# Two QKV groups of the second head pair, issued behind the first two blocks of head 0

## The chip, the cores and the metric

The kernel runs on one core of one Trainium2 chip. The metric is the device time of one execution in microseconds (us); several executions are made, and the median counts. One further execution is recorded by the hardware profiler; its trace gives every instruction of every engine with start and duration, from the first instruction of the program to the last (the span).

The core has five engines that work beside each other, each through its own queue in order: TensorE (PE; its weight loads are listed apart as PEld), VectorE (DVE), ScalarE (ACT), GpSimd (POOL) and SyncE (SP), which here only issues transfers. Matrix products land in PSUM, eight banks of 128 x 512 float32; everything else lies in SBUF.

## The reference

A transformer block on 2048 rows of 1024 features: 16 attention heads of 64 features with rotary positions and a causal mask, then a feed-forward part whose weights come as 4-bit codes with scales.

```
x = L0_attn_hidden_states                       # 1 x 2048 x 1024
x = x + layernorm(attn(layernorm(x), Wq, Wk, Wv, Wo))
x = x + layernorm(ffn(layernorm(x), gate, up, down))

attn(h):  q, k, v = h @ Wq, h @ Wk, h @ Wv      # 16 heads x 64
          q, k = rotary(q), rotary(k)
          p = softmax(causal(q @ k.T) / 8)
          return concat(p @ v) @ Wo
ffn(h):   W = NF4[codes] * scales               # 2752 x 1024, blocks of 64
          return (silu(h @ Wg.T) * (h @ Wu.T)) @ Wd.T
```

## The kernel before

**Precision.** Large products are made of float32 values split into a high part and the rest. `split` writes the high part on ACT (line 120) and the rest on DVE (line 121); `mm3` (lines 112 to 114) issues three matmuls for one product, high x high, high x rest and rest x high. A weight tile is prepared in the same manner by `prep_w`: one transfer into an "f4" buffer (line 179), a scaled cast on ACT (line 186), the rest on DVE (line 190) or POOL.

**Stages.** The 2048 rows are four column blocks c of 512. `make_x` loads, normalizes and transposes one block into four tiles `xs[c]`, and stores them to `xd` for later. A *group* (m, c) is one call of `qkv`: query, key and value (n = 0, 1, 2) of head pair m (heads 2m and 2m + 1) for block c. Each n takes 24 matmuls per 512 columns, three for each of eight row tiles, 72 for the group. The result is copied out of its bank by ACT (line 251, or 241 for the value). Queries and keys are rotated with a table `tab` on DVE and POOL (lines 253 to 256), split into `hl` and stored to `qs` or `ks`; values are transposed on PE (line 244), split into `vo` and stored to `vs`. All stores are issued by SP.

With `ramp=True` a group takes PSUM banks of kind "S" for n = 0 and 2 and "F" for n = 1, and the transfer of `tab` is issued by ACT. Without it all three take the one "F" bank, and SP issues the table. Values are always transposed in "F".

Attention goes head by head. `attend(h, J, ...)` handles 512 queries: `scores` makes J + 1 blocks of 512 keys for each of four tiles of 128 queries (two matmuls each, lines 278 and 280, in a bank of kind "S"), takes the maximum on DVE (284 or 286), the exponential on ACT (288), and scales on POOL (310); `weighted` transposes the probabilities on PE (320), splits them into `pw` and multiplies by v (324, 325). Head 0 loads its k, v and q by parts and goes through J = 0, 1, 2, 3.

**What sets the order.** The order of the instructions on each engine is fixed when the program is built. A planner works with estimated times: of the instructions that are ready, it takes the one that stands first in the program; `early` moves a helper ahead by 1000 places. So a later line of the program runs first only where an earlier one still lacks data, a buffer or a bank. Groups of pairs 2 to 7 fill PE beside attention; during pair 0, heads 0 and 1, these are (2, 0) to (2, 3). They are traced behind both heads, and `pace` ties each product to a score matmul, which it must not precede.

**Buffers.** Each kind has a fixed number: "hd" 7, "w" 3, "xc" 4, "pa" 6, "pb" 2, "f4" 4, "pw" 3, "t2" 3. Blocks 1 and 3 of x lie in "xc", block 2 in four of "hd", block 0 in four of "pa". The weights of pair 0 take the three "w", those of pair 1 two of "pa" and two of "pb". k and v of a head take one "hd" each, and q of two blocks one more. Probabilities of block J take J + 1 of "pa". `tab`, `hl`, `vo` and the raw weights `wf` take "f4"; the copies `t1` and `sh` take "t2".

**Around the change.** Lines 356 to 365 make x and the first eight groups, those of pairs 0 and 1, by `both`. Lines 398 to 401 prepare the weights of pair 2 and load x for (2, 0), ahead of the loop over J of head 0 (line 404). Line 409 takes q buffers for two blocks at a time.

Of the kernel before, what the change touches and what calls it, by code (L numbers as in the profile page):

```python
# [57 lines left out]
def block_kernel(ctx, tc, x, wq, wk, wv, wo, gu_codes, gu_scales, d_codes, d_scales, cos_sin, out):  # L58
# [15 lines left out]
    def slot(tag, shape, dtype, name):  # L74
        assert int(np.prod(shape[1:])) * 4 <= SLOTS[tag][1] * 1024, (tag, shape)
        return sb.tile(shape, dtype, tag=tag, name=name, bufs=SLOTS[tag][0])

    def bank(tag, name="bk"):
        return ps.tile([P, 512], F32, tag=tag, name=name, bufs=BANKS[tag])
# [22 lines left out]
    def f32(ap):  # L102
        return ap.bitcast(F32)

    def after(ins, other):

        dep = mybir.DependencyInfo(mybir.DependencyClass.NoSync, mybir.DependencyReason.DATA)
        tc.add_manual_dep(ins.ins, other.ins.name, dep, reason="pace")

    def mm3(o, w, xx, first, last):  # L110

        r = T.matmul(o, lhsT=w[:, 0], rhs=xx[:, 0], start=first, stop=False)  # L112
        T.matmul(o, lhsT=w[:, 0], rhs=xx[:, 1], start=False, stop=False)  # L113
        T.matmul(o, lhsT=w[:, 1], rhs=xx[:, 0], start=False, stop=last)  # L114
        return r
# [3 lines left out]
    def split(hi, lo, src):  # L119
        high[:] = [A.copy(hi, src)]  # L120
        return V.tensor_tensor(lo, src, f32(hi), ALU.subtract)  # L121
# [96 lines left out]
    def load_x(c):  # L218
        tiles = []
        for kp in range(4):  # L220
            tiles.append(slot("xc", [P, 2, 2, 512], FR, "xc"))
            load(f32(tiles[kp]), xd[c][:, kp])
        return tiles

    def prep_qkv(m, tags=("w", "w", "w")):
        behind = (None, high[-1], high[-1]) if m == 0 else (None,) * 3
        return [prep_w(w, m, sc, tag, b) for w, sc, tag, b in zip((wq, wk, wv), (0.125, 1.0, 1.0), tags, behind)]

    def qkv(m, c, ws, xs, ramp=False, pace=None):
        cs = slice(c * 512, (c + 1) * 512)  # L230
        tab = slot("f4", [P, 2, 512], F32, "tab")
        (A.dma_start if ramp else load)(tab, cos_sin[:, :, cs])
        for n, w in enumerate(ws):
            o = bank("S" if ramp and n != 1 else "F", "qkv")
            for k in range(KE):
                mm = mm3(o, w[k], xs[k // 2][:, :, k % 2, :], k == 0, k == KE - 1)
                if k == 0 and pace:
                    pace(mm, n)
            t1 = slot("t2", [P, 512], F32, "t1")
            if n == 2:  # L240
                A.copy(t1, o)
                pv = bank("F", "pv").rearrange("p (t n) -> p t n", t=4)
                for t in range(4):
                    T.transpose(pv[:, t, :], t1[:, t * P : (t + 1) * P], ident)
                vo = slot("f4", [P, 4, 2, 2, D], FR, "vo")
                src = pv.rearrange("p t (a d) -> p t a d", a=2)
                for a in range(2):
                    split(vo[:, :, a, 0, :], vo[:, :, a, 1, :], src[:, :, a, :])
                load(vs[m][cs].rearrange("(t p) a n -> p t (a n)", p=P), f32(vo.rearrange("p t a l d -> p t (a l d)")))
            else:  # L250
                A.copy(t1, o)
                sh = slot("t2", [P, 512], F32, "sh")
                V.stream_shuffle(sh, t1, [i ^ 1 for i in range(32)])
                V.tensor_tensor(t1, t1, tab[:, 0, :], ALU.mult)
                G.tensor_tensor(sh, sh, tab[:, 1, :], ALU.mult)
                G.tensor_tensor(t1, t1, sh, ALU.add)
                hl = slot("f4", [P, 2, 512], FR, "hl")
                split(hl[:, 0, :], hl[:, 1, :], t1)
                load((qs, ks)[n][m][:, :, cs], f32(hl))
# [71 lines left out]
    def load_kv(h, k, v, cs):  # L331

        m, r = h // 2, h % 2 * D
        for a in range(2):
            load(f32(k[a * D : (a + 1) * D, cs]), ks[m][r : r + D, a, cs])
        load(f32(v[:, cs.start // P : cs.stop // P]), vs[m][cs, h % 2, :].rearrange("(t p) n -> p t n", p=P))

    def load_q(h, q, J):

        m, r = h // 2, h % 2 * D  # L340
        for a in range(2):
            load(f32(q[a * D : (a + 1) * D]), qs[m][r : r + D, :, J * 512 : J * 512 + 512])

    def early(f, *args):
        tc.trace_state.cur_priority -= EARLY
        r = f(*args)
        tc.trace_state.cur_priority += EARLY
        return r

    xs = [early(make_x, 0)]  # L350
    first = [early(prep_qkv, 0), prep_qkv(1, ("pa", "pa", "pb"))]

    def new_x(c):
        xs.append(early(make_x, c))

    def both(*steps):
        for m, c in steps:
            qkv(m, c, first[m], xs[c], ramp=True)
# [3 lines left out]
    new_x(2)  # L362
    both((0, 1), (1, 1))
    new_x(3)
    both((0, 2), (0, 3), (1, 2), (1, 3))

    def new_kv():
        return slot("hd", [P, S], FR, "k"), slot("hd", [P, NT, P], FR, "v")

    def new_q():  # L370

        q = slot("hd", [P, 2, 2, 512], FR, "q")
        return [q[:, 0], q[:, 1]]

    def attend(h, J, q, k, v, anchors):
        weighted(h, J, scores(J, q, k, anchors), v)
# [7 lines left out]
    def group(m, c, xs=None, pace=None):  # L384
        if m not in ws:
            ws[m] = prep_qkv(m)
        qkv(m, c, ws[m], xs or load_x(c), pace=pace)

    for pair in range(KE - 1):
        anchors = []  # L390
        now = [later[g] for g in range(len(later)) if g * (KE - 1) // len(later) == pair]
        own = now and now[0][0] == pair
        for h in (2 * pair, 2 * pair + 1):
            k, v = new_kv()
            by_part = h == 0 or (own and h % 2 == 0)
            if not by_part:
                load_kv(h, k, v, every)
            if h % 2 == 0 and not own:
                if now[0][0] not in ws:
                    ws[now[0][0]] = prep_qkv(now[0][0])  # L400
                ready = load_x(now[0][1])
            order = FIRST if by_part else ORDER
            qj = {}
            for i, J in enumerate(order):
                if by_part:
                    if own and J == now[0][1]:
                        group(*now.pop(0))
                    load_kv(h, k, v, parts[J])
                if i % 2 == 0:
                    two = order[i : i + 2]  # L410
                    qj.update(zip(two, new_q()))
                    for jj in () if by_part else two:
                        load_q(h, qj[jj], jj)
                if by_part:
                    load_q(h, qj[J], J)
                attend(h, J, qj[J], k, v, anchors)
        for i, (m, c) in enumerate(now):

            def pace(mm, n):
                want = PACE * (3 * i + n) / (3 * len(now)) * anchors[-1][0]  # L420
                after(mm, next(a for a in anchors if a[0] >= want)[1])

            group(m, c, None if i or own else ready, pace)
# [416 lines left out]
```

## Time and profile before

| what | us |
|---|---|
| median of three executions | 3017.91 |
| the executions | 3012.16, 3017.91, 3018.10 |
| profiled execution, its own time | 3014.01 |
| its span, first to last instruction | 3012.1 |
| mean granted TensorE clock | 0.991 of full |

Costly groups, from the page (line, engine, operation, output<-inputs, shape, count | busy us, mean ns of one | idle us before them, and what ended most of it):

```profile
L288 ACT ACTIVATE prob<-s,mxs 128x512 f32<-128x512 f32 (+3 forms) x640 | 402.6, 632 | 147.8 <-DVE mxs L286 90.6
...
L320 PE MATMUL pt<-ident,prob 128*128 128x128 f32 x2176 | 345.5, 275 | 6.8 <-DVE pw L121 5.5
...
L286 DVE TENSOR_REDUCE mxs<-s 128x1 f32<-128x512 f32 x384 | 260.9, 681 | 60.0 <-PE s L280 59.1
...
L112 PE MATMUL qkv<-xc,w 128*128 128x512 f32 x576 | 231.8, 402 | 10.3 <-ACT w L186 6.3
```

The operand `qkv<-xc,w` marks the groups whose x was loaded again; the first eight groups read `xr`, the tiles as they were made. Matmuls overlap in PE's pipeline, so the mean duration of one is longer than the distance between two starts. The page divides the span into 40 slices of 75.3 us and gives for each the busy share of each engine in tenths, and the clock that TensorE was granted. The trace further answers for any stretch of time: busy time of each engine, what ended each wait, and the single instructions in order.

### The profile page before, as it was taken

To read this page: it belongs to the slowest core of one execution; us is meant where nothing else is said; L and a number is where in the kernel's file an instruction comes from. 1 tells how busy PE (TensorE), PEld (TensorE's weight loads), DVE (VectorE), ACT (ScalarE), POOL (GpSimd) and SP (SyncE) were. 2 spreads that over 40 slices of the span, in tenths; PEclk is the share of its full clock that TensorE was granted. 3 is DMA by queue.
4 is the path that set the end of the run, shared out by engine and by line. 5 is a ranking of instruction groups with operands and counts; after the bars stand their busy time and mean duration, and the time that the engine had idled before them with its cause. 6 is when DMAs were issued, how large, how long until landed. Compare 5 with 4: busy or idle time off the path is not lost.

```text
span 3012.1 us, 42532 instructions
## 1 busy us (share of the span) xinstructions
PE 2917.0 (97%) x14168; PEld 2409.7 (80%) x14168; DVE 2035.8 (68%) x4171; ACT 1698.4 (56%) x3569; POOL 953.0 (32%) x1055
## 2 busy tenths in 40 slices
PE   7989999999998999999999999999999999999998
PEld 6868888787887787777788788888888887888887
DVE  6567778886777778777665767776666677444347
ACT  4256667776666667667555655655555566333234
POOL 4344344443434343445322121222211223100034
PEclk9999999999999999999999999999999999999999
DMA  8787665757556468463456444444334444744446
GB/s 287 277 249 233 214 222 177 222 161 220 172 195 182 146 202 260 137 210 105 123 187 213 130 134 143 151 133 140 131 119 140 138 153 146 254 141 148 150 144 234
DMA packets 271740, 536.01 MB, mean 178 GB/s; under 512 B 22944, under 2 KB 113056, under 8 KB 255648
## 3 DMA queue, kind: packets, MB, share of 16 engines
q1 hardware_dynamic: 269344, 529.10, 54.6%
q10 hardware_dynamic: 2176, 4.19, 0.4%
q8 instruction: 112, 1.84, 0.3%
q14 instruction: 108, 0.88, 0.1%
HBM read 371.98 MB, written 161.22 MB: 177 GB/s over the span
## 4 chain that ended last, share of the span: by engine, by line
PE 79%; DMA 10%; DVE 4%; ACT 2%; POOL 2%; issue 1%; SPq 1%; POOLq 0%; ACTq 0%; DVEq 0%
PE bk L112 14%; PE bk L114 14%; PE bk L113 14%; PE pt L320 6%; PE qkv L112 4%; PE qkv L113 4%; PE qkv L114 4%; PE o L325 3%; PE o L324 3%; PE s L278 3%; PE s L280 3%; DMA wf<-in_wq 3%; PE pj L469 2%; PE pj L471 2%; PE pj L470 2%
## 5 line engine op out<-in xcount | busy, mean ns | idle before, releaser
L310 POOL TENSOR_SCALAR prob<-prob,rc 128x512 f32<-128x512 f32 (+3 forms) x640 | 405.4, 659 | 436.4 <-DVE rc L305 219.6
L112 PE MATMUL bk<-x,wt 128*128 128x512 f32 x1376 | 534.0, 390 | 2.7 <-ACT wt L120 1.8
L113 PE MATMUL bk<-x,wt 128*128 128x512 f32 x1376 | 535.2, 389 | 0.0
L114 PE MATMUL bk<-x,wt 128*128 128x512 f32 x1376 | 535.1, 389 | 0.0
L288 ACT ACTIVATE prob<-s,mxs 128x512 f32<-128x512 f32 (+3 forms) x640 | 402.6, 632 | 147.8 <-DVE mxs L286 90.6
L121 DVE TENSOR_TENSOR pw<-pt,pw 128x512 fp32r<-128x512 f32 (+3 forms) x640 | 378.4, 602 | 119.7 <-ACT pw L120 118.0
L534 ACT ACTIVATE ln<-cs,bias 128x512 f32<-128x512 f32 x520 | 360.0, 716 | 109.2 <-DVE m L541 25.4
L120 ACT CAST pw<-pt 128x512 fp32r<-128x512 f32 (+3 forms) x640 | 324.1, 527 | 171.6 <-PE pt L320 140.6
L320 PE MATMUL pt<-ident,prob 128*128 128x128 f32 x2176 | 345.5, 275 | 6.8 <-DVE pw L121 5.5
L320 PEld LDWEIGHTS pt<-ident,prob 128*128 128x128 f32 x2176 | 267.6, 141 | 61.7 <-issue 7.2
L112 PEld LDWEIGHTS bk<-x,wt 128*128 128x128 f32 x1376 | 258.2, 188 | 57.5 <-ACT wt L120 2.6
L286 DVE TENSOR_REDUCE mxs<-s 128x1 f32<-128x512 f32 x384 | 260.9, 681 | 60.0 <-PE s L280 59.1
L114 PEld LDWEIGHTS bk<-x,wt 128*128 128x128 f32 x1376 | 258.3, 188 | 53.8
L113 PEld LDWEIGHTS bk<-x,wt 128*128 128x128 f32 x1376 | 258.3, 188 | 53.5
L278 PE MATMUL s<-k,q 128*128 128x512 f32 (+3 forms) x640 | 265.7, 416 | 25.1 <-ACT prob L288 22.4
L325 PE MATMUL o<-pw,v 128*128 128x512 f32 (+3 forms) x640 | 247.3, 388 | 9.5 <-DVE pw L121 9.0
L324 PE MATMUL o<-pw,v 128*128 128x512 f32 (+3 forms) x640 | 244.3, 382 | 9.8 <-ACT pw L120 7.9
L112 PE MATMUL qkv<-xc,w 128*128 128x512 f32 x576 | 231.8, 402 | 10.3 <-ACT w L186 6.3
L113 PE MATMUL bk<-bt,at 128*128 128x512 f32 x616 | 239.6, 389 | 0.0
L114 PE MATMUL bk<-bt,at 128*128 128x512 f32 x616 | 238.8, 389 | 0.0
L112 PE MATMUL bk<-bt,at 128*128 128x512 f32 x616 | 238.7, 389 | 0.0
L280 PE MATMUL s<-k,q 128*128 128x512 f32 (+3 forms) x640 | 236.6, 372 | 0.0
(150 smaller groups left out, 5513.8 us busy)
## 6 DMA issues: line engine op xcount, KB each, us to landing
xc<-xd SPq DMA_DIRECT2D x96, 1024.0 KB, 9.3
q<-qs SPq DMA_DIRECT2D x128, 256.0 KB, 7.2
ast<-S SPq DMA_DIRECT2D x44, 512.0 KB, 3.9
cs<-in_gu_scales SPq DMA_DIRECT2D x172, 128.0 KB, 3.2
cs<-in_gu_codes SPq DMA_DIRECT2D x86, 256.0 KB, 3.0
A<-in SPq DMA_DIRECT2D x66, 256.0 KB, 2.0
S<-in SPq DMA_DIRECT2D x66, 256.0 KB, 3.2
ast<-A SPq DMA_DIRECT2D x33, 512.0 KB, 4.5
```

Source lines behind the costliest of these rows:

```text
L112: r = T.matmul(o, lhsT=w[:, 0], rhs=xx[:, 0], start=first, stop=False)
L113: T.matmul(o, lhsT=w[:, 0], rhs=xx[:, 1], start=False, stop=False)
L114: T.matmul(o, lhsT=w[:, 1], rhs=xx[:, 0], start=False, stop=last)
L121: return V.tensor_tensor(lo, src, f32(hi), ALU.subtract)
L278: mm = T.matmul(s, lhsT=q[:, 0, j * P : (j + 1) * P], rhs=k[:, b:e], start=True, stop=False)
L280: T.matmul(s, lhsT=q[:, 1, j * P : (j + 1) * P], rhs=k[:, b:e], start=False, stop=True)
L288: A.activation(prob[i][:, j, : e - b], s, AF.Exp, bias=mx, scale=sign, accum_out=sums[:, j % BATCH, i : i + 1])
L310: G.tensor_scalar(p, p, rc[:, jj % BATCH, i : i + 1], 0.0, ALU.mult, ALU.add)
L320: T.transpose(pt[:, j * P : (j + 1) * P], prob[kb // 4][:, j, kb % 4 * P : (kb % 4 + 1) * P], ident)
L324: T.matmul(o[:, cs], lhsT=v[:, kb, :], rhs=pw[:, 0, cs], start=kb == 0, stop=False)
L325: T.matmul(o[:, cs], lhsT=v[:, kb, :], rhs=pw[:, 1, cs], start=False, stop=kb == nk - 1)
L534: A.activation(ln, c8, AF.Prelu, bias=bias_of[ab], scale=ab[0], alpha=ab[2])
```

## The change

The groups (1, 2) and (1, 3) are taken out of the last call of `both` and called inside the loop over J of head 0, before its third block. There they are called without `ramp=True`, so that all three products take the "F" bank and SP issues the table.

```diff
@@ -362,7 +362,7 @@
     new_x(2)
     both((0, 1), (1, 1))
     new_x(3)
-    both((0, 2), (0, 3), (1, 2), (1, 3))
+    both((0, 2), (0, 3))
 
     def new_kv():
         return slot("hd", [P, S], FR, "k"), slot("hd", [P, NT, P], FR, "v")
@@ -402,6 +402,10 @@
             order = FIRST if by_part else ORDER
             qj = {}
             for i, J in enumerate(order):
+                if h == 0 and i == 2:
+
+                    for c in (2, 3):
+                        qkv(1, c, first[1], xs[c])
                 if by_part:
                     if own and J == now[0][1]:
                         group(*now.pop(0))
```

The arithmetic and the number of instructions stay as they were.

## The prediction

> **What bounds the kernel now.** I read the page first: busy time, then the forty slices.
>
> ```profile
> PE 2917.0 (97%) x14168; PEld 2409.7 (80%) x14168; DVE 2035.8 (68%) x4171; ACT 1698.4 (56%) x3569; POOL 953.0 (32%) x1055
> ...
> PE   7989999999998999999999999999999999999998
> ...
> PE 79%; DMA 10%; DVE 4%; ACT 2%; POOL 2%; issue 1%; SPq 1%; POOLq 0%; ACTq 0%; DVEq 0%
> ```
>
> TensorE is busy 97% of 3012.1 us, and 79% of the chain of waits is PE. The change removes no arithmetic, so it can only gain where PE stands still or runs at a lowered clock. After the start, the only 8 among the first twelve slices is the fourth (150.6 to 225.9 us). So next I asked for the busy time of the engines in stretches around it (columns: stretch, length, busy us and count of PE, weight loads, DVE, ACT, POOL, granted clock, DMA share, GB/s).
>
> ```profile
> 100.00:168.00 68.00, 67.57 (x316) 55.68 (x314) 25.22 (x52) 17.67 (x41) 23.77 (x16) 1.00 0.79 262
> ...
> 204.00:268.00 64.00, 63.99 (x343) 53.62 (x342) 46.54 (x109) 39.36 (x102) 29.57 (x38) 1.00 0.72 229
> ```
>
> Up to 168 us PE is full of QKV products while DVE works 25 of 68 us. From 204 us on, attention and later QKV groups fill it again. The hole lies between:
>
> ```profile
> 168.00:172.00 4.00, 1.50 (x6) 0.88 (x6) 2.55 (x9) 2.25 (x8) 0.00 (x0) 0.96 1.02 238
> 172.00:176.00 4.00, 4.00 (x11) 2.83 (x12) 1.66 (x7) 1.45 (x4) 1.99 (x4) 0.61 1.14 246
> 176.00:180.00 4.00, 4.00 (x20) 3.28 (x19) 0.00 (x0) 0.30 (x1) 0.10 (x1) 1.00 1.09 271
> 180.00:184.00 4.00, 1.68 (x11) 1.17 (x9) 2.01 (x5) 1.61 (x4) 3.04 (x2) 1.00 1.05 300
> 184.00:188.00 4.00, 3.15 (x11) 2.62 (x12) 4.00 (x9) 2.75 (x9) 2.88 (x2) 0.67 1.07 384
> 188.00:192.00 4.00, 2.77 (x13) 1.95 (x11) 3.44 (x12) 3.43 (x11) 0.00 (x0) 0.91 1.01 416
> 192.00:196.00 4.00, 3.22 (x11) 1.57 (x11) 3.44 (x14) 3.60 (x14) 0.28 (x1) 1.00 1.00 413
> 196.00:200.00 4.00, 3.75 (x20) 2.43 (x19) 3.90 (x15) 3.20 (x11) 3.30 (x7) 1.00 1.08 372
> 200.00:204.00 4.00, 3.91 (x17) 2.73 (x18) 3.69 (x11) 3.72 (x10) 3.22 (x5) 1.00 1.04 351
> ```
>
> Idle here: 2.50 + 0 + 0 + 2.32 + 0.85 + 1.23 + 0.78 + 0.25 + 0.09 = 8.0 us. Twice the clock falls after it (0.61, 0.67). Time lost to the clock is busy time times one minus clock: 1.50 x 0.04 + 4.00 x 0.39 + 3.15 x 0.33 + 2.77 x 0.09 = 2.9 us. So 10.9 us are lost where attention of head 0 begins while QKV work runs out. The timeline of PE shows on whom it waits:
>
> ```profile
> 170.99 0.44 PE L278 MATMUL s<-k,q 128*128 128x384 f32 x1 [1.64 <-ACT prob L288]
> ...
> 184.85 0.50 PE L325 MATMUL o<-pw,v 128*128 128x512 f32 x1 [2.77 <-DVE pw L121]
> ...
> 200.96 0.50 PE L112 MATMUL qkv<-xc,w 128*128 128x512 f32 x1
> ```
>
> Blocks J = 0 and 1 are chains of short steps through four engines (score, maximum, exponential, scaling, transpose, split, product). The first matmul that fills again, of group (2, 0), comes at 200.96 us.
>
> **The change, part by part.** Two groups, (1, 2) and (1, 3), leave the time before attention and follow blocks 0 and 1 of head 0 in program order. Each issues 72 matmuls of L112 to L114, four transposes (L244), on ACT three copies, two casts hl and two casts vo, on DVE two shuffles, two products and four subtractions, on POOL four operations, and four DMAs (tab, qs, ks, vs). All still run: removed work is zero. In the timeline consecutive matmuls of a group start 0.227 us apart, so both are 144 x 0.227 = 32.7 us of PE, now available to cover the chains of blocks 0 and 1. Those hold 4 and 4 + 4 score blocks, 4608 columns, or 9 full blocks of 512. Each full block costs PE two score passes, four transposes and two products, about 4 x 0.227 + 4 x 0.11 = 1.35 us (an estimate; the transposes by 0.82 us for x6 in the timeline). That is 12 us of PE spread over chains that took over 30 us. The gain has a ceiling: the 10.9 us.
>
> Data do not forbid it. The loads of k, v and q for block 0 are issued at 107.96, 109.19 and 116.58 us, those for block 1 up to 144.02 us, and the last product of group (0, 3) is copied at 148.52 us. Attention can start there rather than at 167.68 us.
>
> What is paid back:
>
> First, the banks. As ramp groups the two use four PSUM banks (S three times, F); now F alone. Between two products PE must leave QKV until ACT's copy is done (mean 0.587 us), and after V until copy, transposes and two splits are (0.58 + 0.60 + 2 x (0.37 + 0.42) = 2.8 us). Low bound: zero, since groups (2, 0) onward use the same one bank and the stretch from 204 to 268 us is idle 0.01 us. High bound, nothing else ready: 4 x 0.59 + 2 x 2.8 = 8.0 us. Attention is thinner here (12 of some 45 us of PE, against about half at 204 us), but present, and scores get the three S banks for themselves. I take 2.0 us, a quarter of the high bound, nearer to the row at 204 us because that one shows the same bank at work beside attention.
>
> TensorE: Matmul & The Clock Gate, section "A second HAM failure mode: psum-queue depth-cycling", speaks against this part: small idle times while PSUM banks are cycled make the clock oscillate between full and half. The case's rows show 0.61 and 0.67 only behind 4 us stretches with over 2 us of idleness, and 1.00 behind 0.25 to 0.78 us. If the rule held at each of six handoffs, and each cost the 1.56 us of the first dip, 9.4 us would be added and the gain would vanish; by the rows nothing is added.
>
> Second, the refill. Tiles of x for (1, 3) hold the four "xc" buffers until its last matmul, and only then can the x for (2, 0) load. Before, that load is issued at 180.84 us after the group's end at 179.2 us; the DMA table has 9.1 us to landing. Until then attention is alone, now with the larger block 2. The stretch from 192 to 204 us, attention alone, is idle 1.12 of 12 us. For some 15 us that makes 1.4 us; low bound zero, high bound by the stretch from 184 to 204 us (3.2 idle of 20) 2.4 us.
>
> Third, queues. Tables tab move from ACT's queue to SP's: two issues of 0.55 us off ACT, at nothing, ACT being busy 17.67 of 68 us. On SP they join loads and stores issued in order, among which one sits waiting:
>
> ```profile
> 165.85 9.97 SPq L342 DMA_DIRECT2D q<-qs x4
> ...
> 203.22 4.48 SPq L232 DMA_DIRECT2D tab<-in_cos_sin  x1
> ```
>
> Behind them stand stores ks, vs, the x loads and weights. The weights of pair 2 (three L179 loads into "f4", 13.1, 8.9 and 9.3 us to landing) and the x of (2, 0) are now ahead of the moved groups in program order. A late tab stops DVE (L254) and POOL (L255), and behind DVE's queue the attention. PE's cover is then the next product, 24 x 0.227 = 5.4 us; without cover it is the price of the third rival. Earlier weights are a small help: the first matmul of (2, 0) waited for w, and only until 200.96. I put this part at zero between -1 and +8 us.
>
> Sum: -10.9 + 2.0 + 1.4 + 0 = -7.5 us. Against the profiled execution's span of 3012.1 us that is 3004.6 us; its own time of 3014.0 us becomes 3006.5. The median shown is 3017.9, 3.9 us above that execution, and the runs lie between 3012.2 and 3018.1. I carry the difference to the median: 3010.4, say 3010 us. With all bounds at once (-10.9 - 1 and -10.9 + 8.0 + 2.4) the likeliest case alone lies from 3006 to 3017 us, most of it between 3007 and 3013, since the high bounds would have to meet.
>
> **Rivals.** *The hole only moves.* Blocks 0 and 1 are too thin, all six handoffs stand open (8.0 us) and the refill costs 2.4 us: 10.4 of 10.9 us are given back, 3017 us. For it: the chains left PE idle 2.3 of 4 us even beside other work. Against it: the one-bank groups that run without idleness at 204 us.
>
> *The order does not change.* A planner fixes each engine's order by readiness and program order, and k of head 0 already loads 40 us before the groups it stands behind. If PE still takes the groups first, 3018 us. Against it: with equal readiness the earlier line wins, and attention is now earlier.
>
> *Slower: the tables come late.* Place: SP's queue and the four "f4" buffers, of which three hold weights of pair 2. If each of the two tabs waits 4.5 us on SP and lands 9.7 us later, DVE and POOL stand, and PE runs as from 180 to 192 us, where 4.4 us of idleness and about 1.3 us of clock fall on 12 us, 0.475 per us. Two times 14.2 us cost 13.5 us. With handoffs and refill (4.4) that makes 17.9 against 10.9 recovered: +7.0, 3025 us. It decides once DVE's waits for tab pass some 14 us in all. For it: before the change DVE waited 18.3 us for tab in four waits from 100 to 300 us, one of them ending just ahead of the 2.77 us hole. Against it: the later groups load tab by SP too, without a hole.
>
> **How the numbers follow.** Chances: forecast 0.57, the hole only moves 0.16, order unchanged 0.06, slower 0.21. About 0.2%, 6 us, can be told from no change here, so faster means under 3012. The forecast's case falls there in some five parts of six (0.47), with the rest (0.10) within 0.2%, since its sum lies close to that bound; the two middle rivals lie within 0.2% (0.22); of the slower case four fifths pass 3024 (0.17) and the rest stays within (0.04). That gives 0.47 faster, 0.36 within, 0.17 slower. The range takes in the forecast's bounds, both middle rivals and the near part of the slower one, with some 2 us for spread among runs: 3003 to 3025 us.
>
> **What would show it.** Right: scores of head 0 start near 148 us, between matmuls of (1, 2); idle time from 150 to 210 us falls from 8 to about 4 us and the clock stays at 1.00; (2, 0) starts about 15 us after (1, 3) ends. Handoffs show as PE's waits for ACT's copy L251 or for vo; the slower case as DVE L254 and POOL L255 waiting for tab beside PE idleness and a clock under 0.7. I am wrong if the idle time is gone there but the end has not moved: then later stages, idle 8.7 us from 900 to 1000 us, gave it back.

## The result

The changed kernel takes 3041.06 us (median of four runs, 3039.45 to 3044.89), the kernel before 3017.11 us in the runs beside it: the ratio of the means is 1.0084, 95% interval 1.0070 to 1.0099. It is 24 us slower, where 7.5 us faster was forecast. The profiled execution's span is 3038.8 us, 26.7 us longer than before.

The page after, the same lines as before:

```profile
PE 2923.7 (96%) x14168; PEld 2412.2 (79%) x14168; DVE 2032.8 (67%) x4171; ACT 1696.0 (56%) x3569; POOL 949.4 (31%) x1055
...
PE   7989999999999999998999999999999999999998
...
PE 79%; DMA 10%; DVE 4%; ACT 3%; issue 1%; POOL 1%; SPq 1%; POOLq 0%; ACTq 0%; DVEq 0%
```

The counts are the same to the instruction, and PE's busy time grew by 6.7 us only, 5.2 us of it from a lowered clock. So the time went into waiting. The busy time of the engines in stretches (columns as before: stretch, length, PE, weight loads, DVE, ACT, POOL, granted clock, DMA share, GB/s) shows the first place:

```profile
100.00:140.00 40.00, 39.58 (x190) 32.57 (x189) 17.80 (x42) 13.24 (x35) 12.45 (x10) 1.00 0.86 298
140.00:164.00 24.00, 13.96 (x56) 9.24 (x55) 16.81 (x44) 12.17 (x34) 11.48 (x14) 0.80 0.64 179
164.00:200.00 36.00, 33.56 (x163) 27.12 (x163) 24.11 (x57) 19.14 (x50) 11.95 (x15) 0.99 0.77 191
...
204.00:268.00 64.00, 63.39 (x331) 52.52 (x330) 43.49 (x99) 36.59 (x97) 24.00 (x29) 1.00 0.81 259
```

The hole from 168 to 204 us is filled, but a new one of 10.0 us idle time at a clock of 0.80 stands from 140 to 164 us. The timeline of PE, after, shows what stands in it:

```profile
140.42 0.39 PE L114 MATMUL qkv<-xr,w 128*128 128x512 f32 x1
...
153.61 0.50 PE L278 MATMUL s<-k,q 128*128 128x512 f32 x1 [1.92 <-ACT prob L288]
...
154.61 1.12 PE L244 MATMUL pv<-ident,t 128*128 128x128 f32 x4 [0.20 <-ACT t L241]
157.18 0.90 PE L320 MATMUL pt<-ident,prob 128*128 128x128 f32 x3 [1.46 <-POOL prob L310]
161.47 0.76 PE L278 MATMUL s<-k,q 128*128 128x512 f32 x1 [3.40 <-DMA q<-qs]
163.64 0.73 PE L112 MATMUL qkv<-xr,w 128*128 128x512 f32 x1
```

Between the last product of (0, 3), which starts at 140.42 us, and the first of (1, 2) at 163.64 us there is no QKV matmul at all. Attention did start early, but without the cover that it was meant to get. The `pv` transposes in the middle are the value path of (0, 3) in the F bank, which (1, 2) now needs for its first product. That path ends on DVE:

```profile
157.20 0.42 DVE L121 TENSOR_TENSOR vo<-pv,vo 128x256 fp32r<-128x256 f32 x1
```

So the bank is held until 157.6 us. The last 6 us before 163.64 have another immediate reason: the score products that stand ahead of (1, 2) in PE's fixed order wait 3.40 us for the load of q.

To see where the rest went I cut the span at the ends of the head pairs (the last product of L324 or L325 of each) and added, for each stage, the time in which no matmul runs and the matmul time lost to the clock (busy time times one minus the granted clock). All values in us:

| stage | before | after |
|---|---|---|
| up to the end of pair 0 | 32.0 | 37.4 |
| pair 1 | 1.7 | 17.2 |
| pairs 2, 3, 4 | 7.2, 13.2, 13.1 | 7.9, 10.6, 18.6 |
| pairs 5, 6, 7 | 12.0, 4.9, 15.9 | 12.0, 4.1, 15.2 |
| behind pair 7 | 16.7 | 19.2 |
| sum | 116.7 | 142.2 |

The sum grew by 25.5 us, close to the span's 26.7. A stage's value varies by itself: one experiment below has the same order of work on PE as the kernel before until 1373 us, and its stages differ from it by up to 3.7 us. So the 5.4 us of pair 0 and the 5.5 us of pair 4 are barely clear of that, and no experiment looks into pair 4; the 15.5 us of pair 1 are well clear. Pair 1 as a whole, before and after:

```profile
371.40:526.70 155.30, 153.55 (x848) 128.65 (x847) 120.44 (x307) 106.14 (x278) 69.96 (x93) 1.00 0.61 197
...
361.00:547.90 186.90, 174.64 (x917) 144.39 (x916) 129.45 (x330) 114.79 (x303) 72.26 (x94) 0.97 0.65 201
```

Pair 1 holds none of the moved groups. It is longer partly because more QKV work now falls into it, but PE also stands idle for 12.3 us in it, against 1.8 before. Its holes in the changed kernel:

```profile
370.00:380.00 10.00, 5.43 (x21) 3.73 (x20) 5.70 (x20) 5.49 (x18) 0.00 (x0) 0.83 1.02 354
380.00:390.00 10.00, 9.01 (x43) 6.95 (x42) 9.47 (x27) 8.74 (x22) 7.85 (x12) 0.83 1.07 295
...
430.00:440.00 10.00, 6.56 (x42) 5.61 (x40) 3.16 (x5) 3.40 (x8) 0.00 (x0) 1.00 0.87 275
...
470.00:480.00 10.00, 7.60 (x39) 6.13 (x37) 3.38 (x13) 2.78 (x9) 5.27 (x8) 1.00 1.06 277
```

All three fall between two QKV groups or between two products of one. The largest follows the end of (2, 3) at 366.7 us; (3, 0) starts at 386.9 us. The same turn took from 340.4 to 358.7 us before, where head 1 was still running:

```profile
340.00:360.00 20.00, 17.97 (x108) 14.75 (x107) 16.63 (x42) 15.93 (x43) 3.25 (x6) 1.00 1.05 359
```

There attention, nearly alone, keeps DVE and ACT at 16 to 17 of 20 us and PE at 18. After the change the turn falls on the start of head 2 (head 1 ends at 361.0 us).

The planned order on PE says the same without any time. Counted is how many of the score products (80 in a pair of heads) stand ahead of a group's first product:

| group | (1, 2) | (1, 3) | (2, 0) | (2, 1) | (2, 2) | (2, 3) | (3, 0) | (3, 1) |
|---|---|---|---|---|---|---|---|---|
| before | 0 | 0 | 22 | 38 | 50 | 71 | 94 | 112 |
| after | 15 | 28 | 36 | 51 | 72 | 87 | 111 | 128 |

QKV lags by some 15 score products from the moved groups on, until pair 2.

### The profile page after: what moved, and what is told of

Read it like the earlier page. It is cut to its first block, busy times and chain, and to the rows that moved or that the text cites. A ratio compares the mean times of both kernels' runs of the same rounds, so it can differ in the third digit from the quotient of the medians.

```text
span 3038.8 us, 42510 instructions
## 1 busy us (share of the span) xinstructions
PE 2923.7 (96%) x14168; PEld 2412.2 (79%) x14168; DVE 2032.8 (67%) x4171; ACT 1696.0 (56%) x3569; POOL 949.4 (31%) x1055
## 4 chain that ended last, share of the span: by engine, by line
PE 79%; DMA 10%; DVE 4%; ACT 3%; issue 1%; POOL 1%; SPq 1%; POOLq 0%; ACTq 0%; DVEq 0%
PE bk L114 14%; PE bk L113 14%; PE bk L112 14%; PE pt L320 6%; PE qkv L112 5%; PE qkv L113 4%; PE qkv L114 4%; PE o L325 3%; PE o L324 3%; PE s L278 3%; PE s L280 3%; PE pj L473 2%; PE pj L475 2%; DMA wf<-in_wq 2%; PE pj L474 2%
## 5 line engine op out<-in xcount | busy, mean ns | idle before, releaser
L325 PE MATMUL o<-pw,v 128*128 128x512 f32 (+3 forms) x640 | 248.5, 390 | 6.5 <-DVE pw L121 6.0
L324 PE MATMUL o<-pw,v 128*128 128x512 f32 (+3 forms) x640 | 243.1, 380 | 10.8 <-ACT pw L120 8.4
```

What stands on the lines that cost most here:

```text
L324: T.matmul(o[:, cs], lhsT=v[:, kb, :], rhs=pw[:, 0, cs], start=kb == 0, stop=False)
L325: T.matmul(o[:, cs], lhsT=v[:, kb, :], rhs=pw[:, 1, cs], start=False, stop=kb == nk - 1)
```

## The experiments

Two theories for the first step: the *banks* (the call lost `ramp=True`, and with it the S banks) or the *place* (attention ahead of the groups). Two for the second: the *lag* of QKV makes the holes of pair 1, or something else there does. Each time is a median; in brackets the ratio of the means to the kernel before, run beside it, with its interval.

**Move kept, four banks and ACT's table given back.**

```diff
-                        qkv(1, c, first[1], xs[c])
+                        qkv(1, c, first[1], xs[c], ramp=True)
```

> The moved groups keep their place behind blocks 0 and 1 of head 0, but get the four banks back and ACT issues their table, as before the change. Bank theory (group (1, 2) cannot start while the one F bank is held by the value path of (0, 3), so blocks 0 and 1 run without cover from 141 to 164 us and all later QKV groups are some 26 us late): first product of (1, 2) near 141 us, idle plus clock loss up to the end of pair 0 falls from 37 us to below 30 us, time 3010 to 3020 us. Place theory (attention ahead of the groups is itself what costs, through ACT, DVE and the load queue): time stays within 3033 to 3042 us.

Measured: 3025.02 us (1.0035, 1.0019 to 1.0050). Most of the loss is gone; pair 1 loses 2.0 us. But (1, 2) starts at 154.5 us, not at 141, and the stage up to the end of pair 0 loses 39.6 us, no less than in the changed kernel. The time lies 5 us above what the bank theory gave, 8 us below what the place theory gave.

**Move kept, four banks, table still on SP.**

```diff
-            o = bank("S" if ramp and n != 1 else "F", "qkv")
+            o = bank("S" if (ramp or wide) and n != 1 else "F", "qkv")
...
+                        qkv(1, c, first[1], xs[c], wide=True)
```

> The moved groups get the four banks back, the table is still issued by SP. Bank theory: as with both, 3010 to 3020 us. Table theory (the table joins SP's queue too late and stops DVE and POOL, my third rival): the early holes stay, 3030 to 3041 us, while the run with the table on ACT as well is fast.

Measured: 3023.16 us (1.0025, 1.0014 to 1.0036), pair 1 loses 2.0 us. The same within the intervals as with ACT's table: which queue issues the table makes no difference, and my rival of the late table falls.

**No move, only the lost banks.**

```diff
-    both((0, 2), (0, 3), (1, 2), (1, 3))
+    both((0, 2), (0, 3))
+    for c in (2, 3):
+        qkv(1, c, first[1], xs[c])
```

> Groups (1, 2) and (1, 3) at their old place ahead of attention, but with one bank and SP's table: only the second half of the change. Bank theory: (1, 2) again waits for the value path of (0, 3), with nothing else to run, so at least 8 us of handoffs and the 10 to 20 us late start show, 3025 to 3040 us. Place theory: no more than a few us, 3017 to 3022 us.

Measured: 3038.77 us (1.0074, 1.0054 to 1.0094), nearly the whole loss without any move. PE's timeline of this run:

```profile
161.00 0.77 PE L278 MATMUL s<-k,q 128*128 128x512 f32 x1 [3.23 <-DMA q<-qs]
...
163.16 0.73 PE L112 MATMUL qkv<-xr,w 128*128 128x512 f32 x1
```

Group (1, 2) stands ahead of attention in the program here, and yet starts at 163.16 us, behind 15 score products, as in the changed kernel. Without a bank it is not ready, and the planner takes what is: attention. Once the banks are lost, the move in the program adds little: 1.0074 without it, 1.0084 with it, the intervals overlapping.

**Values of pair 0 transposed in a T bank, in the changed kernel.**

```diff
-                pv = bank("F", "pv")
+                pv = bank("T" if m == 0 else "F", "pv")
```

> The changed kernel with one edit: the values of pair 0 are transposed in a T bank, so that F is free for the first product of (1, 2) as soon as the second product of (0, 3) is copied. Blocked-bank theory (the loss starts because the value path of (0, 3) holds F until 158 us): (1, 2) starts near 141 us, the first hole is covered and the time is 3010 to 3024 us. Rival, narrow-bank theory (the moved groups lose because each of their products waits for the copy of the one before): (1, 2) may start earlier, but QKV still lags by 20 us at (2, 0), time 3032 to 3042 us.

Measured: 3035.86 us (1.0059, 1.0037 to 1.0081), as the narrow-bank theory gave; the interval overlaps that of the changed kernel. Now (1, 2) starts at 137 us, and the first hole shrinks:

```profile
140.00:164.00 24.00, 20.74 (x100) 16.55 (x98) 16.16 (x35) 12.80 (x33) 10.66 (x10) 1.00 0.79 221
164.00:200.00 36.00, 31.80 (x138) 24.85 (x139) 23.81 (x59) 18.99 (x48) 17.43 (x21) 0.86 0.78 206
```

It is idle 3.3 us instead of 10.0, at full clock. So the F bank held by the value path is what kept (1, 2) back. Part of the hole has only moved: behind 164 us PE is now idle 4.2 us instead of 2.4, at a clock of 0.86, and up to the end of pair 0 the run loses 33.8 us instead of 37.4. But (1, 3) still starts only at 176 us (156 before the change), (3, 0) stands behind 110 score products, and pair 1 loses 11.9 us. The blocked first product is the smaller part; the one bank for all six products keeps the lag.

**The same with four banks and ACT's table** (both edits in the changed kernel).

> Move kept, with the four banks, ACT's table and values of pair 0 transposed in a T bank. If the hole at the start of attention can be covered by two QKV groups once no bank stands in the way, (1, 2) starts near 141 us and the time is 3004 to 3012 us, under that before. Rival (the planner puts attention on the S banks first, so that the groups still start late): like the run with four banks alone, 3020 to 3027 us.

Measured: 3016.81 us (0.9995, 0.9984 to 1.0007), between the two expectations. With every bank cleared the move costs nothing and brings nothing: pair 0 loses 39.2 us, though (1, 2) starts at 137 us. There is a new gap of 4.5 us up to 185.7 us, where PE waits for the split of a value group, with a clock of 0.66 in the ten microseconds from 180 us. This looks like my first rival, the hole that only moves, and it needed a different kernel to appear.

**The T bank alone, in the kernel before.**

> The kernel before with one edit: values of pair 0 transposed in a T bank. Control for the runs that combine this with the move: if the bank of the values alone changes nothing, 3014 to 3020 us; if it helps or hurts by itself, more than 4 us off.

Measured: 3023.97 us (1.0028, 1.0016 to 1.0039). Not neutral: the control is 8 us slower by itself, with 37.4 us lost up to the end of pair 0. The planner makes another order from it. Against this control the move gains some 7 us, against the kernel before nothing; I do not call either a property of the move.

**Only (1, 3) moved**, with four banks and the T bank.

> Only (1, 3) is moved behind blocks 0 and 1, with four banks, ACT's table and values of pair 0 in a T bank. If covering the hole needs one group only and the rest of the loss comes from QKV that is held back, 3006 to 3014 us, faster than before. If attention ahead of any QKV group only moves the hole, 3015 to 3024 us.

Measured: 3024.42 us (1.0026, 1.0015 to 1.0038), pair 0 loses 41.5 us. It is no faster than its control with the T bank alone.

**QKV made to lag, in the kernel before.** First from 20, then from 42, then from 36 per cent of pair 0's score work on; the second edit is shown:

```diff
-                want = PACE * (3 * i + n) / (3 * len(now)) * anchors[-1][0]
+                share = (3 * i + n) / (3 * len(now))
+                want = (0.42 + 0.5 * share if pair == 0 else PACE * share) * anchors[-1][0]
```

> The kernel before with one edit: the products of groups (2, 0) to (2, 3) may start only 20 to 85 per cent into the score work of pair 0, instead of 0 to 85 per cent, so that QKV falls behind attention as it does after the change. Lag theory (most of the loss is paid in pair 1, because QKV groups that lag meet the thin start of the next pair and the crowded load queue there): pair 1 loses 8 to 16 us instead of 1.7, time 3025 to 3035 us. Rival (the loss is made where the groups stood and later stages only shift): pair 1 stays below 5 us, time 3017 to 3022 us.

Measured with 20 per cent: 3015.88 us (0.9998, 0.9985 to 1.0011). It was no test. The order on PE stays that of before until 1373 us, (3, 0) behind 94 products, because the groups stood behind that share already. It serves as the control for the spread of the stages.

> The kernel before with one edit: products of (2, 0) to (2, 3) may start only 42 to 92 per cent into the score work of pair 0, so that they now really lag. Lag theory (QKV groups that lag some 26 us cost 10 to 16 us in pair 1, whatever made them lag): (2, 0) starts after 220 us, time 3025 to 3035 us. Rival (a lag alone is harmless): pair 1 loses under 5 us, time 3014 to 3022 us.

Measured with 42 per cent: 3049.34 us (1.0103, 1.0082 to 1.0123). The planned order now has the changed kernel's lag almost to the product ((2, 0) to (3, 0) behind 35, 52, 72, 87 and 111), with all banks and the first eight groups as before. Pair 1 loses 16.0 us, with the same hole at the turn to (3, 0):

```profile
370.00:380.00 10.00, 5.90 (x35) 4.76 (x33) 5.62 (x15) 5.47 (x15) 0.00 (x0) 0.97 1.04 341
380.00:390.00 10.00, 8.54 (x28) 5.88 (x29) 7.82 (x30) 8.00 (x26) 4.98 (x8) 0.69 1.07 318
```

PE is busy 14.4 of 20 us there, as after the change. The time lies above the expected range; pair 0 loses 40.6 us as well, probably because what is held back there is missing as cover.

> The kernel before with QKV of pair 0 held back less at first: (2, 0) behind 30 score products (before 22, run with 42 per cent 35), but (3, 0) behind 110 as in the lagging runs. If the loss of pair 1 follows from where (3, 0) stands, it is 10 to 17 us again and the time 3026 to 3040 us; if it follows from where (2, 0) stands, it is about half, and the time below 3030 us.

Measured with 36 per cent: 3046.05 us (1.0108, 1.0076 to 1.0140). With (2, 0) behind 30 and (3, 0) behind 110, pair 1 loses 13.0 us: it follows (3, 0), not (2, 0). The time lies above the expected 3026 to 3040 us, since pair 0 loses 48.9 us.

**Lag caught up, in the changed kernel.**

```diff
-            group(m, c, None if i or own else ready, pace)
+            (early if pair == 0 else lambda f, *a: f(*a))(group, m, c, None if i or own else ready, pace)
```

> The changed kernel with one edit: the groups (2, 0) to (2, 3) of pair 0 are planned ahead of attention (early), so that the lag of QKV is caught up; in the planned order (3, 0) then stands behind 94 score products again, as before the change, and not behind 111. Bank, start and place of the moved groups stay as changed. Lag theory: pair 1 loses under 4 us instead of 17, time 3022 to 3032 us. Rival (the holes of pair 1 have another cause than the lag): pair 1 still loses 10 us or more, time 3036 to 3044 us.

Measured: 3030.03 us (1.0047, 1.0025 to 1.0069), 11 us below the changed kernel. Banks and the late start of (1, 2) are as changed; (3, 0) is back behind 94 products and pair 1 loses 2.3 us. The turn to (3, 0) in this run:

```profile
352.00:372.00 20.00, 17.50 (x98) 14.39 (x97) 17.01 (x39) 16.00 (x42) 2.09 (x4) 0.93 1.04 340
```

Again DVE at 17 and ACT at 16 of 20 us, as before the change. What remains of the loss is in pair 0, 43.0 us.

All runs so far fall into two groups by that one position:

| (3, 0) behind | pair 1 loses, us |
|---|---|
| 93 to 95 score products (before and 7 runs) | 0.9 to 2.3 |
| 110 to 112 (after and 4 runs) | 10.2 to 17.2 |

**What makes the holes of pair 1.** PE's and ACT's timelines of the changed kernel, at the largest:

```profile
376.52 0.80 PE L278 MATMUL s<-k,q 128*128 128x512 f32 x1 [3.73 <-ACT prob L288]
...
372.11 0.19 ACT L288 ACTIVATION_READ_ACCUMULATOR prob<-s,mxs 128x1 f32 x1
375.08 0.58 ACT L327 COPY ol<-o 64x512 f32<-64x512 f32 x1 [2.78 <-DMA at<-ol]
```

PE waits for an exponential of ACT, and ACT waits for the one buffer `ol`, whose store has not landed; SP's queue had let a table wait 12.80 us ahead of such a store later on. So I issued that store elsewhere:

```diff
-        load(at[J][h * D : (h + 1) * D, :], ol)
+        G.dma_start(at[J][h * D : (h + 1) * D, :], ol)
```

> The changed kernel with one edit: the stores of attention's results (line 329) are issued by POOL instead of SP. Queue theory (in pair 1 ACT stands until the one buffer ol is free, because the store stands in SP's queue behind a table or q load that waits for a buffer): pair 1 loses under 8 us instead of 17, time 3026 to 3034 us. Rival (the store lands late because the transfers themselves are crowded, or the holes have other causes): pair 1 still loses 12 us or more, time 3036 to 3044 us.

Measured: 3059.6 us (1.0136, 1.0117 to 1.0156), outside both expectations. Pair 1 still loses 13.9 us, 3.3 us less than in the changed kernel, which is within the spread of a stage, and ACT's waits there no longer name the store. So SP's queue alone does not make the holes. The test is not clean: the run is 18 us slower than the changed kernel, and POOL, which now issues the store in order, stood 26.7 us in three waits of pair 1.

> The changed kernel with one edit: the query weights of pair 3 are prepared in the free pb buffers, so that (3, 0) need not wait until (2, 3) gives its w buffers back; the planned order on PE in pair 1 stays the same. If PE's wait for weights at the turn from (2, 3) to (3, 0) makes the holes of pair 1, it loses under 10 us instead of 17 and the time is 3028 to 3036 us. If the holes come from attention standing without a QKV product whatever the weights do (order alone), pair 1 still loses 13 us or more, 3037 to 3045 us.

The edit gives `prep_qkv(3)` the tag "pb" for its first weight. Measured: 3039.66 us (1.0076, 1.0061 to 1.0092); pair 1 loses 19.5 us. But the edit hardly brought the weights forward. The issue of the query weights and their cast, in the changed kernel and in this run:

```profile
368.05 0.38 SPq L179 DMA_DIRECT2D wf<-in_wq  x1
385.40 2.31 ACT L186 ACTIVATE w<-wf 128x512 fp32r<-128x512 f32 x4
...
367.20 0.38 SPq L179 DMA_DIRECT2D wf<-in_wq  x1
384.54 2.37 ACT L186 ACTIVATE w<-wf 128x512 fp32r<-128x512 f32 x4
```

The load leaves some 1.5 us after the end of (2, 3) in both and lands some 16 us later, and (3, 0) starts 1.5 us after the cast begins: the turn takes 20.3 us, against 20.2. So this run does not test the weights, although PE's waits in pair 1 name none in either run. In the kernel before it is the same: the load leaves at 341.82 us, the cast begins at 358.05 and (3, 0) starts at 358.7. What differs between the two rows of the table above is where the turn falls. In every run of the first row (3, 0) starts before head 1 ends, in every run of the second behind it, where head 2 has begun.

So what the runs show is that place. Which wait of attention there makes the holes stays open: the store and the weights are not cleanly excluded, and neither are crowded transfers (the DMA share is 0.87 to 1.07 in the holes). A second `ol` buffer and weights that really come earlier would tell; neither was tried.

**Is there something better than both?** Groups beside attention planned early in all pairs of the kernel before (`early(group, ...)`), odd query weights in "pb", and both:

> The kernel before with one edit: the groups beside attention are planned early in all pairs; (3, 0) then stands behind 81 score products (before 94). If QKV further ahead than before helps as QKV further back hurts, the loss of the pairs falls by 5 us or more, 3005 to 3012 us. If the step between 95 and 110 is a threshold with nothing left below it, 3014 to 3020 us.

> The kernel before with one edit: the query weights of every odd pair go into the free pb buffers. If PE's waits for weights at the turns (6.3 us in three waits in all) are what can be had, 3010 to 3014 us; if they are covered by what stands behind them, 3015 to 3019 us.

> The kernel before with both edits, groups beside attention early and odd query weights in pb. If the two gains add, 3002 to 3010 us; otherwise as the better of the two alone.

Measured: 3036.49 us (1.0067, 1.0052 to 1.0082), 3014.46 us (0.9999, 0.9987 to 1.0011) and 3040.05 us (1.0085, 1.0067 to 1.0102). The first and the third lie outside what was expected. The second changes little: the order on PE is that of before in every instruction, and (3, 0) starts 18.0 us after (2, 3) ends, before 18.4. Groups planned earlier in all pairs are as bad as later ones here: in the first run, with (3, 0) behind 81 products, pair 1 loses 4.7 us, pair 5 17.1 (before 12.0) and pair 7 22.4 (before 15.9). In the third pair 1 loses 9.5 us with (3, 0) at the same place, so the position alone does not fix the loss. No version here beats the kernel before.

## Why the prediction was wrong

**Right:** the 10.9 us lost from 168 to 204 us before the change, and that attention's data allow an early start (first scores at 134.7 us, even ahead of the 148 forecast). Right also that no work was added, and that the refill is cheap: (2, 0) starts 9.2 us after (1, 3) ends, and PE is idle 0.1 us from 218 to 228 us, where 1.4 us were priced.

**The step that failed** is "First, the banks", where I took 2.0 us, a quarter of the high bound of 8.0. Measured, the banks cost 16 to 18 us: with the four given back the changed kernel takes 3025.02 and 3023.16 us instead of 3041.06. I priced the handoff from one product to the next inside the moved groups. Two things were missing. The first product of (1, 2) must wait for the bank that the value path of (0, 3) holds until 157.6 us, and then stands behind scores that wait for q: 23 us without QKV from 140.42 to 163.64 us, 10.0 us of them idle. The T bank run shows the wait for the bank; it gives back 5 us of the 24 by the medians, with overlapping intervals. And slow handoffs do not stay where they are: on a single bank, with attention in between, the two groups end at 218 us instead of 180, and every group behind them is late. Bounds made from idle time at the handoffs could not hold that, since the price is paid 150 us later.

**A second term failed: the -10.9 us, booked as recovered in full.** The two runs with the four banks given back do not bring it either. They are 7 to 9 us slower than the kernel before beside them (3016.27 us), and the stage up to the end of pair 0 loses 39.6 and 41.9 us instead of 32.0. The lost time moves: with ACT's table PE stands idle 4.8 us from 140 to 164, 2.1 us from 164 to 200 and 4.7 us from 200 to 230 us. No run realised the gain; why is open.

**The row at 204 us misled me.** It showed one bank at work without idleness, but those groups follow one another 30 us and more apart beside dense attention. Here two groups were to cover thin blocks.

**The lag is the larger part.** Pair 1 accounts for 15.5 of 25.5 us lost; catching up gives back 11 us with banks and start of the moved groups as changed, and a lag alone, in the kernel before, raises the loss of pair 1 from 1.7 to 16.0 us. My section on what would prove me wrong named a loss in later stages, but I had no term for it.

**The rivals.** Slower was given 0.17, but by its own mechanism, the table on SP, it was wrong: with four banks the queue of the table does not matter (1.0025 and 1.0035, intervals overlapping), and in the changed kernel DVE waits 6.6 us for tables from 100 to 300 us, where more than some 14 us were the condition (18.3 before). "The order does not change" was wrong: the order changed, and with the banks lost it changes without the move too.

**The clock.** The prediction set the stated danger of TensorE: Matmul & The Clock Gate, section "A second HAM failure mode: psum-queue depth-cycling" of the Trainium skill, against rows that priced it at nothing. Over the whole span the clock's share of the loss rose from 21.7 to 26.9 us, 5.2 of the 25.5. The clock is low where PE stands idle (0.80 from 140 to 164 us, 0.86 from 164 to 200 in the T bank run); in the changed kernel it is 0.99 from 164 to 200 us, where the one bank is handed from product to product three times. So the page's warning does not show at the handoffs themselves in that row. The dips go with idle time, here mostly in waits of attention; no run separates the two.

Not settled: why the stage up to the end of pair 0 loses 39 to 42 us in all four runs where attention starts early with four banks, against 32 to 36 us in three runs with the order of before.

## What to carry to other kernels

When a call is moved, compare its arguments too: a flag that chooses banks can weigh more than the place. Before work is counted as cover, ask what its first instruction waits for, and who holds that buffer at that moment. Where a planner orders the work, look in the planned order at where the units behind the edit now stand against the next stage: a lag that costs nothing at the edit can be paid where cover is next thin. And before a run is taken as a test, look in its trace whether the edit moved what it was meant to move.

## What was not expected of the hardware

An issue on POOL takes 0.58 us, but the run with the 64 stores of line 329 on POOL was 18 us slower than the one with them on SP. Its waits of 9.4, 9.0 and 8.3 us stand in POOL's own queue, ahead of attention's scaling and the rotary operations; how much of the 18 us is theirs was not separated from the changed order.
